# Two window rows mixed in one step, softmax in place, and a plan that counts tiling changes (layer of window attention, linear attention and a recurrent scan)

## The chip, the cores and the metric

The kernel runs on one core of a Trainium2 chip. The core has TensorE (PE in the profile; its weight loads are PEld), VectorE (DVE), ScalarE (ACT), GpSimd (POOL) and SyncE (SP), which here only issues DMAs. SBUF is the on-chip memory; PSUM is the small memory that TensorE writes to. The metric is the device time of one execution in microseconds (us); the time before is the median of three runs.

## What is computed

The input is 16 images of 56 x 56 positions with 128 channels, in fp32. Cut to what matters:

```python
# layer 0: shifted-window attention on the group-normed image
x = x + L0(gn(x))      # roll by -3; qkv; 8 x 8 windows of 7 x 7; 4 heads of 32;
                       # softmax(q k * scale + bias + mask) v; w_out, b_out; roll back
# layer 1, attention part: causal linear attention over the 3136 tokens of an image
q, k = elu(q) + 1, elu(k) + 1
num = einsum(q, cumsum(k v^T));  den = einsum(q, cumsum(k)) + 1e-6
x = x + num / den      # of the layer-normed tokens
# layer 1, ffn part: batch norm over all tokens of (ln(x) @ W.T), then a scan over tokens
y_t = sigmoid(wx_t + y_{t-1} @ V.T)
out = x + y
```

## The kernel before

**Layout.** An image is 3136 tokens. Window attention works on window rows: 7 image rows, 8 windows of 49 positions, all 4 heads; 8 rows an image, 128 in all, in the order 7, 0, 1, ..., 6 (U_ORDER). Linear attention and ffn work on token groups: 6 groups of 512 tokens and one of 64 for each image. The scan at the end runs over all images at once, with 32 segments for each image, and reads what the groups left in DRAM.

**The plan.** Everything before the scan is a list of steps, each with an engine, a cost (busy time, and time until its result may be used), a rank, the steps that it follows, and the buffers that it takes and drops. Plan.run is a list scheduler: each engine takes the ready step of lowest rank whose buffers are free. emit runs it forwards and backwards 200 times with ranks from the run before, keeps the shortest result and writes the instructions out in that order. On the chip each engine follows its own fixed list, with semaphores between engines. The scheduler has one rule on tiled matmuls, which are those that use a part of TensorE's array (scores and mix): while TensorE's last step was a tiled one, another ready tiled step is taken first if its rank lies within NEAR of the lowest ready rank, and entering tiled work from other work adds SWITCH (0.1 us) to a step's cost.

**A window row** (window_row, from L845). ScalarE gathers and normalises the row into x_bufs (L851); TensorE makes q and k (L864) and v (L885), which ScalarE copies out (L869, L878, L897; v has 2 buffers). Scores (L909) are 32 products for each row, of 32 x 49 by 49, each two instructions in fp32, into one of two PSUM pairs (tag "a"). VectorE adds mask and bias into a buffer s (L920, two buffers) and takes maxima (L932), GpSimd subtracts them (L935), ScalarE writes the exponentials to p_bufs (L945, two, chosen by the row's number), VectorE sums (L949, L951), GpSimd scales (L954). TensorE turns the result in eight transposes (L964, step turn), ScalarE copies it to pT (L974, one buffer, 904 elements a partition including gaps). Mix (L983) is 32 products of 49 x 32 by 49, two instructions each. mix_out (L1018) copies the result into oT (one buffer for an image) in four copies, eight where the row wraps around the image's edge. Scores of a row wait for the turn of the row two before.

**A token group** (token_group, from L1210). It needs the window rows that cover its tokens (need, L1576): TensorE projects them (L1234), VectorE adds to the image in xt_bufs (L1243). layer_scale (L1077) normalises tokens. To turn them so that channels lie on partitions, through_dram writes the group to DRAM and reads it back in four pieces in another order (L1058, L1072, SyncE's queue), and VectorE transposes 32 x 32 blocks (L1139); blocks_moved (L1048) says which groups go this way, and the others use TensorE's transposes (L649) and a copy on ScalarE (L1135). There are three such exchanges for a group: the input of the attention ("a"), its keys ("k", L1348 or L1340 and L1344) and the input of the ffn ("f"). Then come features (L1269 to L1292), values (L1317), products (L1372), the running state (L1412, L1424), the attention itself (L1401, L1404), division (L1482) and the update (L1490).

**Start.** Image 0 is turned by TensorE as its groups arrive. Images from 1 on are loaded in another order into the buffer spare (load_turned, load_blocks, L335) in four DMAs; each of them follows the one before it.

Of the kernel before, what the change touches and what calls it, by code (L numbers as in the profile page):

```python
# [15 lines left out]
WS = 7  # L16
# [25 lines left out]
class Step:  # L42


    def __init__(self, engine, cost, rank, emit, after, takes, drops, lag):
        self.engine, self.cost, self.rank, self.emit = engine, cost, rank, emit
        self.takes, self.drops, self.lag = takes, drops, lag
        self.tiles = False
        self.then = []
        self.missing = 0  # L50
        for a in after:
            if a is not None:
                a.then.append(self)
                self.missing += 1


class Plan:
# [11 lines left out]
    SWITCH = 0.1  # L69
    NEAR = 3.0  # L70
# [17 lines left out]
    def run(self, missing, then, rank, gate, begin=None, done=None):  # L88
# [17 lines left out]
        while events:  # L106
# [14 lines left out]
            for e, steps in ready.items():  # L121
                if busy[e]:
                    continue
                held, best = [], None
                if tiles.get(e):
                    near = sorted(r for r in steps if self.steps[r[1]].tiles)
                    for r in near:
                        if r[0] > min(steps)[0] + self.NEAR:
                            break
                        s = self.steps[r[1]]  # L130
                        if begin is None or begin(s):
                            best = s
                            steps.remove(r)
                            heapq.heapify(steps)
                            break
                while steps and best is None:
                    r = heapq.heappop(steps)
                    s = self.steps[r[1]]
                    if begin is None or begin(s):
                        best = s  # L140
                    else:
                        held.append(r)
                for r in held:
                    heapq.heappush(steps, r)
                if best is None:
                    continue
                busy[e] = True
                start[best.n] = t
                more = self.SWITCH if best.tiles and not tiles.get(e) else 0.0
                tiles[e] = best.tiles  # L150
                push(t + more + best.cost, "idle", best)
                push(t + more + best.lag + self.HOP, "done", best)
# [82 lines left out]
def tile_conv_attn_hybrid(  # L235
# [145 lines left out]
    mean_sb = front.tile([P, P], F32, name="mean_sb")  # L381
    nc.gpsimd.memset(mean_sb, 1.0 / C)
    pb_sb = front.tile([P, WT], F32, name="pb_sb")
# [35 lines left out]
    awc_sb = front.tile([P, 3 * P], F32, name="awc_sb")  # L419
# [10 lines left out]
    with ExitStack() as s1:  # L430
# [46 lines left out]
        for i in range(2):  # L477
# [32 lines left out]
        for xt in xt_bufs:  # L510
# [14 lines left out]
                "v": 2,  # L525
                "s": 2,
                "pT": 1,
# [100 lines left out]
        def load_turned(b, rank):  # L628
# [3 lines left out]
            for q in range(4):  # L632
# [6 lines left out]
                        [issued, *parts[-1:]],  # L639
# [193 lines left out]
        last_turn = [None, None]  # L833
# [3 lines left out]
        def window_row(b, u, i, o, t, taken, normed, xw_buf, oT_buf, rank):  # L837
# [4 lines left out]
            kT, v, s, pT = Buf("kT"), Buf("v"), Buf("s"), Buf("pT")  # L842
            asc, apt, apa = Buf("a"), Buf("a"), Buf("a")
            qT = q_bufs[i % 2]
            pr = p_bufs[i % 2]  # L845
# [71 lines left out]
            def masked():  # L917
                d["s"] = own(s, P, 2, NW, WT)
                mask = wmask_sb[:, 1 if u == NU - 1 else 0]
                nc.vector.tensor_tensor(  # L920
                    d["s"].rearrange("p h w k -> p h (w k)"),
                    d["sc"][:, :, 0:UT],
                    mask.rearrange("p w k -> p (w k)")
                    .unsqueeze(1)
                    .to_broadcast([P, 2, UT]),
                    ALU.add,
                )
                d["sf"] = d["s"].rearrange("p h w k -> p (h w) k")

            def maxima():  # L930
                d["mx"] = small.tile([P, nb], F32, tag="mx", name=f"mx_{n}")
                nc.vector.tensor_reduce(d["mx"], d["sf"], AX.X, ALU.max)  # L932

            def minus():
                nc.gpsimd.tensor_tensor(  # L935
                    d["sf"],
                    d["sf"],
# [4 lines left out]
            prf = pr.rearrange("p h w k -> p (h w) k")[:, :, 0:WT]  # L942

            def expo():
                nc.scalar.activation(prf, d["sf"], AF.Exp)  # L945

            def sums():
                d["sm"] = small.tile([P, nb], F32, tag="sm", name=f"sm_{n}")
                nc.vector.tensor_reduce(d["sm"], prf, AX.X, ALU.add)  # L949
# [3 lines left out]
            def scaled():  # L953
                nc.gpsimd.tensor_tensor(  # L954
                    prf, prf, d["rc"].unsqueeze(2).to_broadcast([P, nb, WT]), ALU.mult
# [3 lines left out]
            def turn():  # L959
                pt = pairs[apt.place].rearrange("p h (w q) -> p h w q", w=NW // 2)  # L960
                d["pt"] = pt
                for hp in range(2):
                    for w2 in range(NW // 2):
                        nc.tensor.transpose(  # L964
                            pt[:, hp, w2, 0:NQ2],
                            pr[0:NQ2, hp, 2 * w2 : 2 * w2 + 2, :].rearrange(
# [5 lines left out]
            def turn_out():  # L972
                d["pT"] = own(pT, P, 2, NW // 2, P)
                nc.scalar.copy(d["pT"][..., 0:NQ2], d["pt"][..., 0:NQ2])  # L974

            def mix():
                pa = pairs[apa.place]
                d["pa"] = pa
                for w2 in range(NW // 2):
                    for h in range(HEADS):  # L980
                        for par in range(2):
                            a = 64 * par
                            nc.tensor.matmul(  # L983
                                pa[HD * h : HD * (h + 1), par, w2 * WT : (w2 + 1) * WT],
                                d["v"][a : a + WT, w2, HD * h : HD * (h + 1)],
                                d["pT"][
                                    a : a + WT, h // 2, w2, 64 * (h % 2) : 64 * (h % 2) + WT
                                ],
                                start=True,
                                stop=True,  # L990
                            )

            def mix_out():
# [9 lines left out]
                for par in range(2):  # L1003
                    src = d["pa"][:, par, 0 : UT // 2].rearrange(
                        "p (w i j) -> p w i j", w=NW // 2, i=WS
                    )
                    for i0, y0, m in row_parts(u):
# [13 lines left out]
            xk = st("ACT", (0.48, 0.59), rank, gather_windows, [*taken, *normed, last_value[i % 2]], drops=[xw_buf])  # L1021
# [7 lines left out]
            sc = st("PE", (0.88, 0.95), rank, scores, [q, k, last_turn[i % 2]], takes=[asc], drops=[kT])  # L1029
            last_score[i % 2] = sc  # L1030
            m = st("DVE", (0.88, 0.97), rank, masked, [sc, None if b else made["mask"]], takes=[s], drops=[asc])
            m = st("DVE", (0.87, 0.96), rank, maxima, [m])
            m = st("POOL", (1.47, 1.51), rank, minus, [m])
            e = st("ACT", (0.77, 0.88), rank, expo, [m], drops=[s])
            m = st("DVE", (1.17, 1.26), rank, sums, [e])
            m = st("POOL", (1.48, 1.52), rank, scaled, [m])
            tu = st("PE", (0.77, 0.94), rank, turn, [m], takes=[apt])
            last_turn[i % 2] = tu
            tu = st("ACT", (0.81, 0.92), rank, turn_out, [tu], takes=[pT], drops=[apt])
            mi = st("PE", (0.74, 0.81), rank, mix, [tu, vo], takes=[apa], drops=[pT, v])  # L1040
            sc.tiles = mi.tiles = True
            cost = (0.91, 1.04) if u < NU - 1 else (1.47, 1.65)
# [5 lines left out]
        def blocks_moved(key, b, g):  # L1048

            return key in KEYS and b < B - 1 and g < NG - 1  # L1050
# [26 lines left out]
        def layer_scale(t, g, d, key, rank, after, to, drops=()):  # L1077
# [79 lines left out]
            if blocks:  # L1157
# [3 lines left out]
                    (0.59, 0.68),  # L1161
# [48 lines left out]
        def token_group(b, g, i, t, turned_x, rows_done, oT_buf, xt_buf, rank):  # L1210
# [140 lines left out]
            if blocks_moved("k", b, g):  # L1351
# [4 lines left out]
                    (0.59, 0.68),  # L1356
# [136 lines left out]
            s = st("ACT", part(g, (0.90, 1.00), (0.22, 0.32)), rank, divided, [s], drops=[apn])  # L1493
            up = st("POOL", part(g, (1.02, 1.08), (0.36, 0.42)), rank, update, [s, scaled], drops=[A])
# [65 lines left out]
        for b in range(B):  # L1560
# [7 lines left out]
            for s, u in enumerate(U_ORDER):  # L1568
                rows[u] = window_row(
                    b, u, b * NU + s, o, t, taken, normed, xw_buf, oT_buf, base + SLOT * s  # L1570
                )
            ups, xss, projects = [], [], []
# [417 lines left out]
```

## Time and profile before

| what | us |
|---|---|
| median of 3 runs (lowest, highest) | 1659.29 (1656.67, 1663.87) |
| the profiled execution | 1664.5 |
| its span, first to last instruction | 1661.4 |
| scores, L909: matmul records, mean of one | 8192, 206 ns |
| mix, L983: matmul records, mean of one | 8192, 211 ns |
| turn, L964: records, mean of one | 1024, 261 ns |
| turn_out, L974: copies, mean | 128, 927 ns |
| mix_out, L1018: copies, busy time | 576, 90.9 us |
| mean granted clock of TensorE | 0.994 |

Records of tiled matmuls overlap, so a count times a mean is not the time that a step takes; that is read from the starts of steps in the timeline. The ordinary copies of mix_out are 196 elements (344 ns), 147 (313 ns), 21 (220 ns) and 28 (209 ns) a partition. Busy times of the engines are shares of the whole span; the scan uses TensorE, ScalarE and VectorE in another way than the part before it, so stretches have to be looked at apart.

### The profile page before, as it was taken

The page shows a single profiled execution, that of the slowest core. Times are in us where ns is not written, and L with a number is a line of the kernel's source. Part 1 is how long each engine was busy: PE and PEld are TensorE (multiplying, and loading weights), DVE is VectorE, ACT ScalarE, POOL GpSimd, SP SyncE. Part 2 cuts the span into 40 slices and gives each one's busy share as a digit, 9 for nine tenths or more (in the row PEclk, how much of TensorE's full clock was granted, in tenths as well). Part 3 has the DMA queues.
Part 4 walks back from the last instruction along what each step waited for, and adds up shares of the span by engine and source line. Part 5 has one row for each costly group of instructions (what it writes and reads, how often), then busy time and mean ns, then how long its engine had stood idle before and what let it go on. Part 6 is the DMA issues. An engine that isn't in the chain of part 4 may idle for free.

```text
span 1661.4 us, 63385 instructions
## 1 busy us (share of the span) xinstructions
PE 1615.4 (97%) x25458; PEld 1308.8 (79%) x25459; DVE 1398.1 (84%) x3044; ACT 1183.5 (71%) x3156; POOL 1272.0 (77%) x2154
## 2 busy tenths in 40 slices
PE   7899999999999999999999999999999999999997
PEld 6678787887878887878888778878888887876876
DVE  5779987897989888987979798978898786757997
ACT  5577776777777777777677777767677776766765
POOL 6788978897989898888989889878889786770000
PEclk9999999999999999999999999999999999999999
DMA  5486767677677768586766777776755655558999
GB/s 137 109 186 158 192 151 172 187 167 208 154 204 166 199 153 206 149 208 169 194 165 156 204 168 196 167 191 156 196 148 155 159 160 147 190 183 342 403 419 379
DMA packets 776720, 322.03 MB, mean 194 GB/s; under 512 B 400481, under 2 KB 760161, under 8 KB 774625
## 3 DMA queue, kind: packets, MB, share of 16 engines
q1 hardware_dynamic: 774832, 317.10, 69.9%
q8 instruction: 202, 3.31, 0.9%
q10 hardware_dynamic: 1584, 0.79, 0.2%
q14 instruction: 102, 0.83, 0.2%
HBM read 171.54 MB, written 146.24 MB: 191 GB/s over the span
## 4 chain that ended last, share of the span: by engine, by line
PE 69%; POOL 8%; DVE 7%; SPq 5%; DMA 5%; issue 3%; ACT 2%; DVEq 0%; POOLq 0%; ACTq 0%
PE bank L864 8%; PE bank L1269 8%; PE bank L885 5%; PE pair L909 5%; PE state_bank L1412 4%; PE pair L964 4%; PE pair L1401 4%; PE bank L1317 4%; PE pair L1404 4%; PE bank L1502 4%; PE bank L1372 4%; PE pair L983 4%; SPq L1072 4%; PE bank L1234 4%; PE z_buf L1785 2%
## 5 line engine op out<-in xcount | busy, mean ns | idle before, releaser
L954 POOL TENSOR_TENSOR p_buf<-p_buf,rc 128x784 f32<-128x784 f32 x128 | 194.4, 1519 | 42.7 <-DVE rc L951 14.2
L1269 PE MATMUL bank<-xnT,awc_sb 128*128 128x512 f32 (+1 forms) x448 | 212.9, 557 | 3.3 <-DVE xnT L1139 2.7
L935 POOL TENSOR_TENSOR s<-s,mx 128x784 f32<-128x784 f32 x128 | 192.2, 1502 | 30.8 <-DVE mx L932 28.5
L1279 ACT ACTIVATE r<-bank,bqk_neg 128x512 f32<-128x512 f32 (+1 forms) x224 | 143.4, 640 | 76.9 <-PE bank L1269 67.3
L1412 PEld LDWEIGHTS state_bank<-v_buf,k 128*128 128x128 f32 x768 | 125.4, 191 | 52.1 <-issue 26.7
L1292 DVE SCALAR_TENSOR_TENSOR f<-bank,bqk_one,r 128x512 f32<-128x512 f32 (+1 forms) x224 | 147.5, 658 | 12.6 <-ACT r L1288 12.1
L1412 PE MATMUL state_bank<-v_buf,k 128*128 128x129 f32 x768 | 155.4, 284 | 1.3 <-ACT state L1424 1.1
L974 ACT COPY pT<-pair 128x904 f32<-128x904 f32 x128 | 118.7, 927 | 51.0 <-PE pair L964 41.3
L1401 PE MATMUL pair<-state,f 128*128 128x129 f32 x768 | 153.1, 281 | 0.6 <-issue 0.6
L1424 ACT COPY state<-state_bank 128x129 f32<-128x129 f32 x384 | 107.0, 279 | 65.5 <-PE state_bank L1412 63.9
L1401 PEld LDWEIGHTS pair<-state,f 128*128 128x128 f32 x768 | 123.4, 192 | 37.0 <-issue 21.8
L920 DVE TENSOR_TENSOR s<-pair,wmask_sb 128x784 f32<-128x784 f32 x128 | 122.7, 958 | 34.2 <-PE pair L909 30.0
L909 PEld LDWEIGHTS pair<-kT,q_buf 32*49 32x49 f32 x8192 | 106.4, 121 | 41.9 <-issue 15.7
L949 DVE TENSOR_REDUCE sm<-p_buf 128x16 f32<-128x784 f32 x128 | 121.6, 950 | 18.6 <-ACT p_buf L945 18.3
L1223 POOL TENSOR_TENSOR xt_buf<-xt_buf,bout_sb 128x512 f32<-128x512 f32 (+1 forms) x112 | 129.1, 1158 | 10.7 <-DMA xt_buf<-in_x_dram 10.5
L1788 ACT ACTIVATE y_a<-z_buf,bsh 128x256 f32<-128x256 f32 (+1 forms) x218 | 103.0, 473 | 47.4 <-PE z_buf L1785 43.3
L1288 ACT ACTIVATE r<-r 128x512 f32<-128x512 f32 (+1 forms) x224 | 131.9, 589 | 2.4
L1785 PE MATMUL z_buf<-y_a,fvT_sb 128*128 128x256 f32 (+1 forms) x432 | 131.0, 389 | 0.4 <-ACT y_a L1788 0.4
L909 PE MATMUL pair<-kT,q_buf 32*49 32x49 f32 x8192 | 122.8, 206 | 2.8 <-issue 2.4
L964 PE MATMUL pair<-ident,p_buf 113*128 113x113 f32 x1024 | 120.9, 261 | 3.1 <-POOL p_buf L954 2.8
L964 PEld LDWEIGHTS pair<-ident,p_buf 113*128 113x128 f32 x1024 | 107.5, 142 | 20.5 <-issue 11.2
L932 DVE TENSOR_REDUCE mx<-s 128x16 f32<-128x784 f32 x128 | 121.5, 949 | 0.9
(170 smaller groups left out, 4697.1 us busy)
## 6 DMA issues: line engine op xcount, KB each, us to landing
x_d<-xt_buf SPq DMA_DIRECT2D x96, 256.0 KB, 2.6
xt_buf<-in_x_dram SPq DMA_DIRECT2D x93, 256.0 KB, 3.2
spare<-in_x_dram SPq DMA_DIRECT2D x60, 392.0 KB, 4.5
xs_d<-staged SPq DMA_DIRECT2D x15, 1568.0 KB, 6.9
xna_d<-spare SPq DMA_DIRECT2D x90, 256.0 KB, 2.7
xnk_d<-f SPq DMA_DIRECT2D x90, 256.0 KB, 3.0
xnf_d<-spare SPq DMA_DIRECT2D x90, 256.0 KB, 2.8
spare<-xna_d SPq DMA_DIRECT2D x256, 64.0 KB, 2.1
```

The costliest lines, as they stand in the source:

```text
L864: nc.tensor.matmul(d[key], wqkv_sb[:, j * P : (j + 1) * P], xk, start=True, stop=True)
L909: nc.tensor.matmul(sc[64 * hh : 64 * hh + WT, hp, w * WT : (w + 1) * WT], qT[r : r + HD, w * WT : (w + 1) * WT], d["kT"][r : r + HD, w * W ...
L935: nc.gpsimd.tensor_tensor(d["sf"], d["sf"], d["mx"].unsqueeze(2).to_broadcast([P, nb, WT]), ALU.subtract,)
L954: nc.gpsimd.tensor_tensor(prf, prf, d["rc"].unsqueeze(2).to_broadcast([P, nb, WT]), ALU.mult)
L964: nc.tensor.transpose(pt[:, hp, w2, 0:NQ2], pr[0:NQ2, hp, 2 * w2 : 2 * w2 + 2, :].rearrange("p w k -> p (w k)"), ident[0:NQ2, 0:NQ2],)
L1269: nc.tensor.matmul(d[f"p{j}"], awc_sb[:, j * P : (j + 1) * P], d["xT"][:, :nt], start=True, stop=True,)
L1279: nc.scalar.activation(d[f"r{j}"], d[f"p{j}"], AF.Relu, bias=bqk_neg[:, j : j + 1], scale=-1.0,)
L1288: nc.scalar.activation(d[f"r{j}"], d[f"r{j}"], AF.Exp, scale=-1.0)
L1292: nc.vector.scalar_tensor_tensor(d[key][:, :nt], d[f"p{j}"], bqk_one[:, j : j + 1], d[f"r{j}"], ALU.add, ALU.max,)
L1401: nc.tensor.matmul(to, chunk(d["f0"], cc), t["states"][c], start=True, stop=False)
L1412: nc.tensor.matmul(t["pd"], d["k"][:, cc, :], v1[:, cc, :], start=c == 0, stop=True, skip_group_check=True,)
L1785: nc.tensor.matmul(z, fvT_sb, y_prev, start=False, stop=True, skip_group_check=True)
```

## The change

- **Mix.** Rows are taken in pairs in the order of U_ORDER: (7, 0), (1, 2), (3, 4), (5, 6). The first row of a pair ends with its turn_out; the mix step of the second does both rows, 128 matmul instructions, and writes the two rows' results side by side, so that mix_out copies both at once (pair_parts joins rows that are neighbours in the image). pT gets 2 buffers, v 4. A group that needs the first row of a pair waits for the pair.
- **Softmax in place.** The buffers s are gone. Mask and bias are added into a p buffer; maxima, subtraction, exponential, sums and scaling all work there. There are 3 p buffers, given out by the plan, dropped at the turn. The rule that scores wait for the turn two rows before is gone.
- **turn and turn_out.** The turned pieces are ordered by pair of heads and window pair, and turn_out copies 2 x 49 of each 113 columns, 784 elements a partition. The turn step takes pT.
- **Plan.** tiles becomes 0, 1 (scores) or 2 (mix). ENTER 0.1, LEAVE 0.22 and CHANGE 0.17 replace SWITCH; NEAR goes from 3 to 6, and steps of the same kind come first. Costs of several steps are set anew.
- **Image 0's first two groups** are turned by TensorE for all three keys and not through DRAM.
- **Image 1's four turned loads** no longer follow each other.
- **Room.** mean_sb and pb_sb lie in staged before its first use; awc_sb lies in the unused last 384 columns of xt_bufs[0].

```diff
-    SWITCH = 0.1
-    NEAR = 3.0
+    ENTER, LEAVE, CHANGE = 0.1, 0.22, 0.17
+    NEAR = 6.0
...
-                    near = sorted(r for r in steps if self.steps[r[1]].tiles)
-                    for r in near:
-                        if r[0] > min(steps)[0] + self.NEAR:
-                            break
+                    near = sorted(
+                        (self.steps[r[1]].tiles != tiles[e], r)
+                        for r in steps
+                        if self.steps[r[1]].tiles
+                        and r[0] <= min(steps)[0] + self.NEAR
+                    )
+                    for _, r in near:
...
-                more = self.SWITCH if best.tiles and not tiles.get(e) else 0.0
-                tiles[e] = best.tiles
+                was, tiles[e] = tiles.get(e, 0), best.tiles
+                more = 0.0
+                if was != best.tiles:
+                    more = self.CHANGE if was and best.tiles else self.LEAVE
+                    more = more if was else self.ENTER
...
-        for i in range(2):
+        for i in range(3):
             pb = keep.tile([P, 2, NW, 64], F32, name=f"p_buf{i}")
...
-                "v": 2,
-                "s": 2,
-                "pT": 1,
+                "v": 4,
+                "p": 3,
+                "pT": 2,
...
-                        [issued, *parts[-1:]],
+                        [issued, *(parts[-1:] if b > 1 else [])],
...
+        def pair_parts(u0, u1):
+
+            parts = []
+            for r, u in enumerate((u0, u1)):
+                for i0, y0, m in row_parts(u):
+                    if parts and sum(parts[-1][1:]) == y0:
+                        parts[-1] = (*parts[-1][:2], parts[-1][2] + m)
+                    else:
+                        parts.append((WS * r + i0, y0, m))
+            return parts
...
             def turn_out():
-                d["pT"] = own(pT, P, 2, NW // 2, P)
-                nc.scalar.copy(d["pT"][..., 0:NQ2], d["pt"][..., 0:NQ2])
+                d["pT"] = own(pT, P, NW, 2, WT)
+                nc.scalar.copy(
+                    d["pT"],
+                    d["pt"].rearrange("p n (h q) -> p n h q", h=2)[..., 0:WT],
+                )
...
+                for r, e in enumerate((first_of["d"], d)):
+                    for w2 in range(NW // 2):
+                        for h in range(HEADS):
+                            for par in range(2):
+                                a, c = 64 * par, WT * (2 * w2 + r)
+                                nc.tensor.matmul(
+                                    pa[HD * h : HD * (h + 1), par, c : c + WT],
+                                    e["v"][a : a + WT, w2, HD * h : HD * (h + 1)],
+                                    e["pT"][
+                                        a : a + WT, NW // 2 * (h // 2) + w2, h % 2, :
+                                    ],
+                                    start=True,
+                                    stop=True,
+                                )
...
-            xk = st("ACT", (0.48, 0.59), rank, gather_windows, [*taken, *normed, last_value[i % 2]], drops=[xw_buf])
+            xk = st("ACT", (0.63, 0.73), rank, gather_windows, [*taken, *normed, last_value[i % 2]], drops=[xw_buf])
...
-            sc = st("PE", (0.88, 0.95), rank, scores, [q, k, last_turn[i % 2]], takes=[asc], drops=[kT])
+            sc = st("PE", (0.77, 0.92), rank, scores, [q, k], takes=[asc], drops=[kT])
             last_score[i % 2] = sc
-            m = st("DVE", (0.88, 0.97), rank, masked, [sc, None if b else made["mask"]], takes=[s], drops=[asc])
+            m = st("DVE", (0.88, 0.97), rank, masked, [sc, None if b else made["mask"]], takes=[p], drops=[asc])
...
-            tu = st("PE", (0.77, 0.94), rank, turn, [m], takes=[apt])
-            last_turn[i % 2] = tu
-            tu = st("ACT", (0.81, 0.92), rank, turn_out, [tu], takes=[pT], drops=[apt])
-            mi = st("PE", (0.74, 0.81), rank, mix, [tu, vo], takes=[apa], drops=[pT, v])
-            sc.tiles = mi.tiles = True
-            cost = (0.91, 1.04) if u < NU - 1 else (1.47, 1.65)
+            tu = st("PE", (0.77, 0.94), rank, turn, [m], takes=[apt, pT], drops=[p])
+            tu = st("ACT", (0.72, 0.83), rank, turn_out, [tu], drops=[apt])
+            sc.tiles = 1
+            if i % 2 == 0:
+                first_rows[i] = {"d": d, "u": u, "after": [tu, vo], "drops": [pT, v]}
+                return None
+            first_of = first_rows[i - 1]
+            mi = st(
+                "PE",
+                (1.28, 1.43),
+                rank,
+                mix,
+                [tu, vo, *first_of["after"]],
+                takes=[apa],
+                drops=[pT, v, *first_of["drops"]],
+            )
+            mi.tiles = 2
+            cost = (1.27, 1.42) if first_of["u"] < NU - 1 else (1.90, 2.05)
             return st("ACT", cost, rank, mix_out, [mi], takes=[oT_buf], drops=[apa])
...
-            return key in KEYS and b < B - 1 and g < NG - 1
+            return key in KEYS and b < B - 1 and (b or g >= 2) and g < NG - 1
...
-            up = st("POOL", part(g, (1.02, 1.08), (0.36, 0.42)), rank, update, [s, scaled], drops=[A])
+            up = st("POOL", part(g, (1.22, 1.28), (0.42, 0.48)), rank, update, [s, scaled], drops=[A])
...
+                if s % 2:
+                    rows[U_ORDER[s - 1]] = rows[u]
```

## The prediction

> **What bounds the kernel now.** I read the page's head first, then the busy time by stretches, then TensorE's timeline in the middle of the run, then the chain of waits.
>
> ```profile
> span 1661.4 us, 63385 instructions
> ...
> PE 1615.4 (97%) x25458; PEld 1308.8 (79%) x25459; DVE 1398.1 (84%) x3044; ACT 1183.5 (71%) x3156; POOL 1272.0 (77%) x2154
> ...
> PE   7899999999999999999999999999999999999997
> ```
>
> TensorE has no open time after the second slice. The table of stretches splits the run; the columns are the stretch, its length and the busy time of PE, PEld, DVE, ACT and POOL, with the clock, the DMA share and GB/s last:
>
> ```profile
> 83.00:1411.00 1328.00, 1314.28 (x22314) 1069.01 (x22316) 1141.13 (x2562) 971.88 (x2652) 1141.92 (x1916) 1.00 0.70 175
> 1411.00:1487.00 76.00, 74.94 (x924) 62.64 (x914) 53.23 (x130) 53.03 (x148) 56.51 (x113) 1.00 0.57 192
> 1487.00:1661.00 174.00, 158.63 (x904) 124.11 (x904) 148.67 (x257) 111.90 (x245) 12.96 (x32) 0.97 0.93 374
> ```
>
> For 1328 us TensorE is 99% busy at full clock, VectorE and GpSimd are 86% busy, ScalarE 73%. The last 174 us are the scan, which the change leaves as it is. A busy TensorE can still be a slow one, so I took the time from the start of each of its steps to the start of the next and compared it with the shortest seen for the same step between the same neighbours: from 83 to 1411 us the excess is only 30 us. In the chain of waits from 600 to 700 us nearly every piece is PE. The length of the middle is therefore the sum of TensorE's steps, and an edit counts by what it does to them.
>
> TensorE's timeline shows what a tiled step (scores, L909; mix, L983) costs. Columns: start, time to the end of the last record, engine, line, operation.
>
> ```profile
> 601.78 1.02 PE L1502 MATMUL bank<-xfT,fwTc_sb 128*128 128x512 f32 x2
> 602.73 0.95 PE L909 MATMUL pair<-kT,q_buf 32*49 32x49 f32 x64
> 603.61 0.49 PE L1317 MATMUL bank<-awc_sb,xnT 128*128 128x128 f32 x2
> 603.94 0.39 PE L1412 MATMUL state_bank<-v_buf,k 128*128 128x129 f32 x2
> ...
> 611.12 1.02 PE L1502 MATMUL bank<-xfT,fwTc_sb 128*128 128x512 f32 x2
> 611.98 0.39 PE L1401 MATMUL pair<-state,f 128*128 128x129 f32 x2
> 612.20 0.39 PE L1404 MATMUL pair<-v_buf,A 128*128 128x129 f32 x2
> ...
> 613.09 0.38 PE L1412 MATMUL state_bank<-v_buf,k 128*128 128x129 f32 x2
> 613.40 0.81 PE L983 MATMUL pair<-pT,v 49*32 49x49 f32 x64
> 614.14 1.16 PE L1317 MATMUL bank<-awc_sb,xnT 128*128 128x128 f32 x8
> 615.13 0.82 PE L864 MATMUL bank<-x_buf,wqkv_sb 128*128 128x392 f32 x2
> ...
> 660.73 0.95 PE L909 MATMUL pair<-kT,q_buf 32*49 32x49 f32 x64
> 661.60 0.81 PE L983 MATMUL pair<-pT,v 49*32 49x49 f32 x64
> 662.34 1.12 PE L1269 MATMUL bank<-xnT,awc_sb 128*128 128x512 f32 x2
> ```
>
> Read starts only. L1502 takes 0.86 us ahead of a whole step (611.12 to 611.98) and 0.95 ahead of scores: entering costs 0.09. Scores take 0.88. The step behind, two L1317 matmuls, takes 0.33 where two such matmuls (0.89 for eight) take 0.22: leaving costs 0.10. A mix takes 0.74 between the same edges. Where a mix follows scores at once (661.60), scores keep 0.88 (0.87 here by rounding), the mix 0.74, and one entry and one exit are gone. Over all steps in order, the 256 tiled steps stand in 212 stretches: 28 times a mix follows scores, 16 times scores follow a mix. So a stretch costs 0.196 us over its steps, and 212 of them 42 us.
>
> **The change part by part.**
>
> *Two rows in one mix.* The matmuls stay (64 a row), but 128 steps become 64. Within one mix the records start 6 ns apart for the first 32, then pause, and the last 30 start 8.5 ns apart; 133 ns pass from the last start to the next step. No mix of 128 is in the trace. Low end of the saving: the second row costs a whole 0.74, saving nothing. High end: all of it at 6.3 ns, 0.40 us, saving 64 x 0.34 = 21.6 us. I take the pace of the second half, 64 x 8.5 ns = 0.54, because the first burst looks like a queue that fills once: 64 x 0.20 = **-12.5 us**.
>
> *Fewer stretches.* 192 tiled steps remain. Without any merging there are 192 stretches, saving 20 x 0.196 = 4 us; if every stretch held two steps, 96, saving 23 us. Before, 44 of 256 steps were merged (17%) with a window of 3 us in the plan; it becomes 6 us and the same kind is taken first. I take 52 merges of 192 (27%): 140 stretches, 72 x 0.196 = **-14 us**.
>
> The Trainium skill (TensorEngine Tiling (Array Packing), Key Properties) says that changing the tiling mode drains TensorE, and scores (32 rows by 49 columns) and mix (49 by 32) are different modes, so by this rule putting them side by side would save little. The 28 places where a mix follows scores show no charge beyond the scores' usual 0.88 us; by the rule only the 64 vanished steps would count, 64 x 0.196 = 12.5 us instead of 14, so the sum hardly moves.
>
> *ScalarE.* An ordinary mix_out has copies of 344, 313, 220 and 209 ns, 1.09 us by row; one for two rows, of double width, has about 505 (the 392-wide kT copy is 492), 420, 235 and 230, 1.39: 0.8 us less a pair, 50 us in all. turn_out moves 784 elements, not 904: from 927 ns towards 825 (the slope between 512 elements at 594 and 904 at 927), between 0 and 13 us less. I count **nothing**: ScalarE is 73% busy and TensorE's steps cover it. If that cover were gone, up to 60 us would come off ScalarE's own 972.
>
> *Softmax in place, buffers.* Reading the strided p_buf costs VectorE no more (sums 950 ns against maxima 949) and GpSimd 17 ns (1519 against 1502), 2 us over 128 rows. The strided write by the mask's sum is not in the trace; between nothing and, by that GpSimd pair, 1%, 1.2 us. Both are under TensorE's cover. The rule that scores of row i wait for the turn of row i-2 goes; masked waits for the turn of row i-3, and behind it on VectorE stand the other groups' steps. Turn now needs a free pT on TensorE itself, but what frees it is an earlier mix on the same engine, so no foreign wait is added there. **0**, within the stalls below.
>
> *Start.* Six exchanges through DRAM vanish (two groups, three keys): 30 DMA issues from SyncE's queue, 6 x (0.4 + 2.0) = 14 us of it, and in their place 24 transposes and 6 copies: 24 x 0.11 = 2.7 us of TensorE, 3.6 of ScalarE. The four loads of the turned image 1 no longer wait for each other:
>
> ```profile
> 18.80 3.17 SPq L335 DMA_DIRECT2D spare<-in_x_dram  x1
> 48.11 0.39 SPq L1058 DMA_DIRECT2D xna_d<-spare  x1
> 50.52 2.02 SPq L1072 DMA_DIRECT2D spare<-xna_d  x4
> 52.58 0.43 SPq L335 DMA_DIRECT2D spare<-in_x_dram  x1
> ```
>
> One of them stands at 18.80, the next shown at 52.58, and image 1's first transposes (L683) come at 68. TensorE is open for 15.5 of the first 83 us; 7 of its excess lie there, the rest before any row exists. Bounds: +3 (transposes on a full engine) to -7. I take **-3**.
>
> *Plan costs and stalls.* The new costs are nearer to the records (update 1.22 against 1.16 measured where it had 1.02; gather 0.63 against 0.75, had 0.48), which could take some of the 30 us of stalls: low end -10. Against it, VectorE keeps its work while the middle shrinks by 25: its idle time falls from 187 to 162 us, 13%, and by the same share the stalls grow by **+4**. High end +20.
>
> Sum: -12.5 - 14 - 3 + 4 = -25.5, so 1661.4 becomes 1636 in the profiled span. That execution took 1664.5 in all and the median of the runs is 1659.29; I take the difference off the median: **1634**. The terms' own ends, not all at once, give 1623 to 1643.
>
> **Rivals.**
>
> *The output buffer waits for the pair (slower).* There is one oT buffer; its first copy for an image comes 0.3 to 6.4 us after the last projection of the one before in images 4 to 15 (743.5 to 750.0 for image 8). With pairs the first copy needs the image's second row too, and that row's turn came 10, 9 and 7 us after the release in images 7 to 9. If TensorE ran out of other work for 3 us at each of 15 boundaries, 45 us would be lost: 1634 + 45 = 1679. It decides from 25.5 / 15 = 1.7 us a boundary. Against it: the first projection of an image needs the second row before as well, and it started 16 to 22 us after the release; v goes from 2 to 4 buffers and p to 3, so rows can run ahead. 12%.
>
> *Hidden behind VectorE and GpSimd.* Both reach 88% of a shorter middle, in order; new stalls eat all but a few us: 1656, within 0.5%. For it: seven pieces of 1.5 us of GpSimd's p_buf (L954) are among the longest pieces of the chain. Against: nearly all of the chain in the middle is TensorE. 6%.
>
> *Half.* The double mix keeps its burst-and-pause twice (saving near 0) and merges stay at 17% (159 stretches, 10.4 us): -10.4 - 3 + 4, 1649. 15%.
>
> *More.* As forecast, and the truer costs halve the 30 us of stalls: -25.5 - 4 - 15, 1615. This also covers better merging. 12%.
>
> **How the numbers follow.** The forecast has 55%. Faster by over 0.5% (8.3 us, about what a measurement of this kernel tells from no change): 55 + 15 + 12 = 82%; within: 6%; slower: 12%. From 1616 to 1654 lie the forecast, the half case and part of the other two.
>
> **What would show it.** Mix in 64 steps of 128 at 1.28 us from start to start; about 140 stretches of tiled steps; ScalarE's mix copies 320 instead of 576 and its busy time near 1125; the middle 22 to 25 us shorter with TensorE still at 99%; image 1's first transposes before 60 us. A mix at 1.45, stretches over 170, or TensorE's stalls over 50 us would make it wrong, and gaps of more than 2 us at each image's boundary would show the first rival.

## The result, and the profile after

The changed kernel takes 1667.52 us (median of 14 runs) where the kernel before takes 1662.76 us (14 runs beside it): a ratio of 1.0032, with a 95% interval of 1.0017 to 1.0047. The change makes the kernel a little slower, by about 5 us. The forecast was 1634 us, 25 us faster.

The head of the profile page after looks as the one before did: span, busy time by engine, TensorE's slices.

```profile
span 1664.3 us, 63157 instructions
...
PE 1602.6 (96%) x25483; PEld 1309.3 (79%) x25483; DVE 1393.3 (84%) x3038; ACT 1161.8 (70%) x2906; POOL 1273.8 (77%) x2155
...
PE   8999899999999999999999999999999999999997
```

TensorE is busy for 13 us less, and the span is 3 us longer. The table of stretches says where the open time is (columns as in the prediction):

```profile
83.00:1411.00 1328.00, 1296.05 (x22059) 1060.72 (x22058) 1134.07 (x2541) 942.81 (x2395) 1139.31 (x1908) 0.99 0.69 172
1411.00:1487.00 76.00, 75.29 (x1067) 63.94 (x1066) 53.33 (x129) 54.48 (x150) 56.78 (x113) 1.00 0.58 194
1487.00:1661.00 174.00, 159.53 (x923) 124.98 (x921) 149.97 (x263) 113.31 (x251) 15.03 (x38) 0.98 0.94 376
```

In the middle TensorE stood open for 13.7 us before and 32.0 now, and its clock is 0.99 where it was 1.00. No other engine took over: VectorE and GpSimd are less busy too. The list of TensorE's waits after (engine, line, what was waited for, total us, times, longest) names the new open time:

```profile
PE pair L925 <- issue: 16.0, 8, 5.2
PE pair L1002 <- issue: 8.8, 7, 2.8
PE bank L655 <- DMA xt_buf<-in_x_dram: 4.4, 1, 4.4
PE pc L1938 <- DVE seam_count L1934: 3.5, 1, 3.5
```

L925 is scores and L1002 the mix. Before, the mix had no "issue" in this list, and scores (L909) had 2.4 us:

```profile
PE pair L909 <- issue: 2.4, 3, 1.0
```

The third and fourth line were there before (4.5 and 3.5 us). "Issue" is time for which no semaphore and no other engine answers. TensorE's timeline shows where it falls, inside a step:

```profile
186.82 1.02 PE L1300 MATMUL bank<-xnT,xt_buf 128*128 128x512 f32 x2
187.68 1.05 PE L1403 MATMUL bank<-f,f 128*128 128x128 f32 x8
188.57 0.39 PE L1265 MATMUL bank<-wout_sb,oT_buf 128*128 128x128 f32 x2
188.89 1.38 PE L1002 MATMUL pair<-pT,v 49*32 49x49 f32 x128
190.20 0.57 PE L925 MATMUL pair<-kT,q_buf 32*49 32x49 f32 x31
195.99 0.98 PE L925 MATMUL pair<-kT,q_buf 32*49 32x49 f32 x33 [5.22 <-issue]
196.90 2.08 PE L1300 MATMUL bank<-xnT,xt_buf 128*128 128x512 f32 x2
198.77 1.75 PE L901 MATMUL bank<-wqkv_sb,x_buf 128*128 128x128 f32 x8
```

A scores step stops after 31 of its 64 matmuls, all of whose operands are there, for 5.2 us. It follows a mix of 128. And the steps behind it go at half speed: L1300 takes 1.87 us from start to start where it took 0.86 ahead of the gap (186.82 to 187.68), L901 1.58 instead of 0.89. The trace has the granted clock (the share of full speed at which TensorE is let run) at one half for 6.8 us from 193.4 on; in this row, third number from the end, the first 0.4 us are still at full speed:

```profile
193.00:197.00 4.00, 1.01 (x34) 0.92 (x34) 0.00 (x0) 0.00 (x0) 1.74 (x3) 0.55 0.75 217
```

A lack of instructions would stop an engine without a semaphore, and the profile has a queue for these (packets, MB, share of 16 engines' time; the line reads the same before and after):

```profile
q8 instruction: 202, 3.31, 0.9%
```

202 packets of 3.31 MB are 16 KB each. TensorE's records of all kinds (matmuls, weight loads, semaphores) number 51,215, which makes 254 a packet. I take a packet for a page of 256 instructions, and the next count bears that out. Counting the records in order, all 15 gaps over 0.35 us inside tiled steps come at the same place, number 193 modulo 256, and so do the 3 of before. This place is called the border of a page here. At this one place the gaps (over 0.25 us, ahead of the scan) sum to 33.0 us after and 7.3 before; at all other places of a tiled step there is next to nothing.

That gives the theory which the experiments test. *TensorE's instructions come in pages of 256, and only one page ahead.* In the trace a fetch starts a median of 0.9 us after a border is crossed (in a quarter of the cases before it, by up to 2.7 us), takes 1.05 (0.88 to 1.6), and TensorE can cross the next border 1.23 to 1.40 us after the fetch has landed. That floor holds throughout: in the traces of the two kernels and of all runs below, some 200 borders in each, no border was crossed sooner than 1.19 us after that landing. It makes a median of some 3.4 us (5 to 95%: 0.9 to 5.4) from one border to the earliest crossing of the next. Most pages last longer than that: 173 of 199 in this trace took over 3.5 us, and 4 of these had a gap over 0.3 us behind them; of the 26 faster ones 16 had. A pair's mix is 256 instructions (128 matmuls and as many weight loads) in 1.31 us, a page by itself, and scores behind it make 384 in 2.2 us. Sixteen pages of after hold mix and scores alone and last under 1.7 us; 23.7 us of gaps stand behind them. Before had two such pages, and 0.1 us. Taking each gap as "landing of the fetch plus 1.3 us, less the time at which the page before is used up" gives 30.6 us for after where 31.3 are measured in the 17 gaps above 0.3 us, and 5.4 for before where 5.7 are; it is this measure of the gaps that is given for every run below.

The Trainium skill (Runtime: NRT & Kernel Launch, Instruction fetch mechanics) also has refills of 256 instructions, and calls crossing a border "mostly hidden". The size agrees with the 202 packets of 16 KB; "hidden" held for before (5.7 us) and does not hold here (31.3).

### The profile page after: what moved, and what is told of

The parts are those of the page before. It is cut to its first block, busy times and chain, and to the rows that moved or that the text cites. A ratio compares the mean times of both kernels' runs of the same rounds, so it can differ in the third digit from the quotient of the medians.

```text
span 1664.3 us, 63157 instructions
## 1 busy us (share of the span) xinstructions
PE 1602.6 (96%) x25483; PEld 1309.3 (79%) x25483; DVE 1393.3 (84%) x3038; ACT 1161.8 (70%) x2906; POOL 1273.8 (77%) x2155
## 3 DMA queue, kind: packets, MB, share of 16 engines
q8 instruction: 202, 3.31, 0.9%
## 4 chain that ended last, share of the span: by engine, by line
PE 77%; DVE 6%; POOL 6%; DMA 4%; issue 4%; SPq 2%; ACT 0%; DVEq 0%; POOLq 0%; ACTq 0%
PE bank L880 9%; PE bank L1300 9%; PE bank L901 6%; PE pair L925 6%; PE pair L979 5%; PE state_bank L1443 5%; PE bank L1265 5%; PE pair L1432 5%; PE bank L1403 5%; PE bank L1348 5%; PE pair L1435 5%; PE pair L1002 5%; PE bank L1533 4%; PE z_buf L1818 2%; DVE z_buf L1806 2%
## 5 line engine op out<-in xcount | busy, mean ns | idle before, releaser
L949 POOL TENSOR_TENSOR p_buf<-p_buf,mx 128x784 f32<-128x784 f32 x128 | 194.5, 1520 | 42.6 <-DVE mx L946 30.1
L1300 PE MATMUL bank<-xnT,xt_buf 128*128 128x512 f32 (+1 forms) x448 | 212.5, 557 | 2.3 <-DVE xnT L1170 0.8
L937 DVE TENSOR_TENSOR p_buf<-pair,wmask_sb 128x784 f32<-128x784 f32 x128 | 122.9, 960 | 36.4 <-PE pair L925 32.2
L925 PEld LDWEIGHTS pair<-kT,q_buf 32*49 32x49 f32 x8192 | 106.7, 120 | 47.0 <-issue 32.2
L925 PE MATMUL pair<-kT,q_buf 32*49 32x49 f32 x8192 | 123.8, 206 | 16.0 <-issue 16.0
L989 ACT COPY pT<-pair 128x784 f32<-128x784 f32 x128 | 104.8, 818 | 32.1 <-PE pair L979 31.2
L957 ACT ACTIVATE p_buf<-p_buf 128x784 f32<-128x784 f32 x128 | 113.2, 884 | 14.0 <-POOL p_buf L949 13.4
```

The costliest lines, as they stand in the source:

```text
L925: nc.tensor.matmul(sc[64 * hh : 64 * hh + WT, hp, w * WT : (w + 1) * WT], qT[r : r + HD, w * WT : (w + 1) * WT], d["kT"][r : r + HD, w * W ...
L949: nc.gpsimd.tensor_tensor(d["prf"], d["prf"], d["mx"].unsqueeze(2).to_broadcast([P, nb, WT]), ALU.subtract,)
L1300: nc.tensor.matmul(d[f"p{j}"], awc_sb[:, j * P : (j + 1) * P], d["xT"][:, :nt], start=True, stop=True,)
```

## The experiments

Rivals of this theory: the stall belongs to the mix and scores themselves (operands, ports, the change of tiling), or the new order of steps is worse for some other reason. What tells them apart is moving the borders while the order stays, and the order while the steps stay. Ratios are to the kernel before, measured beside each run.

**The same order, borders moved by 64 instructions.** 32 small matmuls are put ahead of the plan.

```diff
+        for _ in range(32):
+            nc.tensor.matmul(state_bank, ident16[:, 0:P], ident16[:, 0 : C + 1], start=True, stop=True)
```

> Edit: 32 matmuls in bf16 ahead of the first load's arrival, 64 instructions of TensorE more, in time that it idles; the plan and the order of all else are those of the changed kernel. Theory F: the borders of 256 instructions fall 64 instructions earlier in the program, so other steps stall; every gap over 0.35 us inside a tiled step is again at one and the same position modulo 256, and the sum of the border gaps is anywhere between 15 and 45 us: 1650 to 1680. Rival P: the same steps stall as in the changed kernel, and the time is 1667 within 3 us.

1659.56 us, ratio 0.9982 (0.9959 to 1.0004). The gaps moved to other steps, and all 17 inside tiled steps are at number 193 again. Their sum stays, 31.0 us. The time at half clock ahead of the scan fell from 27.3 to 20.5 us, which makes at most 3.4 us; the rest of the difference to after is not explained.

**Borders moved by 200.**

```diff
+        for _ in range(100):
+            nc.tensor.matmul(state_bank[:, 0:2], ident16[:, 0:P], ident16[:, 0:2], start=True, stop=True)
```

> Edit: the changed kernel's order, with 100 two-column bf16 matmuls at the start, borders 200 instructions earlier; the first transposes may start 1 to 3 us late. Theory F: the replay over the changed kernel's starts gives 45 to 63 us of gaps, the worst position, against 28 to 38 unmoved: 1667.5 + 20 + 2 = about 1690, ratio 1.017. Rival P: 1667 to 1671, ratio 1.004.

1710.29 us, ratio 1.0254 (1.0212 to 1.0296). Nothing differs but 100 matmuls of two columns, and the kernel is 43 us slower than after. Its waits of TensorE:

```profile
PE pair L931 <- issue: 27.9, 11, 4.9
PE pair L1008 <- issue: 18.6, 14, 2.5
```

Gaps sum to 59.8 us, as expected, and some 68 us ahead of the scan run at half clock; the time is 20 us above the 1690 expected, which had put too little on the clock. Where a border lies in a step decides, so the steps' operands don't.

**Scores and mixes kept apart.** A step that is not tiled is taken after a tiled one.

```diff
-                        (self.steps[r[1]].tiles != tiles[e], r)
+                        (0, r)
                         for r in steps
-                        if self.steps[r[1]].tiles
+                        if not self.steps[r[1]].tiles
```

> Edit: after a tiled step the plan looks for a step that is not tiled, where the changed kernel looks for another tiled one. Tiled steps then stand in 191 stretches instead of 167: 24 x 0.196 = +4.7 us of TensorE work. Theory F (instruction supply: TensorE loses time where its instruction stream crosses a border of 256 instructions, because pages of nothing but tiled matmuls are used up in about 1.4 us, faster than the next page comes): the gaps at those borders fall from 33 us to under 10, and the time at half clock that follows long gaps from 27 us to about 10, so 1667.5 + 4.7 - 23 - 6 = about 1643, ratio 0.988 to the kernel before. Rival P (the loss is in the new order: waits on VectorE, GpSimd or the oT buffer): nothing falls, 1667.5 + 4.7 = 1672, ratio 1.006.

1654.02 us, ratio 0.9950 (0.9927 to 0.9972). With 191 stretches of tiled steps in place of 167 the kernel is faster than before, if by half a percent. That merging, meant to save, costs isn't shown by it alone: the same order with the borders elsewhere gains nothing (below). And gaps of 21.3 us are left, more than was expected, with one merge left of 25: a pair's mix has as many instructions as a page without any merge.

**The same edit in the kernel before.** There `near` is `sorted(r for r in steps if not self.steps[r[1]].tiles)`.

> Edit: the kernel before with the same rule as in apart (after a tiled step one that is not tiled). Stretches go from 212 to 252: 40 x 0.196 = +7.8 us. Theory F: border gaps, 7.3 us before, fall below 4, half clock a little less: 1662.8 + 7.8 - 4 - 2 = about 1665, ratio 1.001. Rival P: 1662.8 + 7.8 = 1671, ratio 1.005.

1677.56 us, ratio 1.0101 (1.0069 to 1.0132): a miss, slower than either. Its gaps are 9.8 us, more than the 5.7 of before and not less, and its 252 stretches cost by count 40 x 0.196 = 8 us more than 212. That makes some 12 of the 16 us. The theory had the direction of the gaps wrong here, at a size of 4 us.

**The start as before.** Image 0's first groups go through DRAM again and image 1's loads follow each other, the rest as after.

```diff
-                        [issued, *(parts[-1:] if b > 1 else [])],
+                        [issued, *parts[-1:]],
...
-            return key in KEYS and b < B - 1 and (b or g >= 2) and g < NG - 1
+            return key in KEYS and b < B - 1 and g < NG - 1
```

> Edit: of the changed kernel, image 0's first two groups go through DRAM again and image 1's four loads follow each other again; the rest stays (the plan comes out in another order, with 160 stretches). Theory F: with 32 adjacent tiled steps instead of 25 the border gaps are 33 x 32/25 = about 42 us, less 7 x 0.196 = 1.4 us of work; the first 83 us hold 4 us less TensorE work, as before the change: 1667.5 + 9 - 1 + 4 = about 1679, ratio 1.010. Rival P: the start alone counts, 1667.5 + 4 - 1 = 1670.

1694.91 us, ratio 1.0215 (1.0162 to 1.0268). That is beyond both expectations. The planner found another order, 13 us longer by its own reckoning (1467 us against 1454), with 49.7 us of gaps and 44 us at half clock. It says nothing on the start alone, and shows how much a new order can move the gaps.

**One mix a row, the rest of the change kept.**

```diff
-                for r, e in enumerate((first_of["d"], d)):
+                for r, e in ((0, d),):
...
-            mi = st("PE", (1.28, 1.43), rank, mix, [tu, vo, *first_of["after"]], takes=[apa], drops=[pT, v, *first_of["drops"]])
+            mi = st("PE", (0.63, 0.78), rank, mix, [tu, vo], takes=[apa], drops=[pT, v])
```

> Edit: the changed kernel with the pairing alone undone, a mix and a mix_out for each row as before; softmax in place, buffers, plan rules, start and costs stay. 214 stretches instead of 167 (+9 us) and the second row's full price (64 x 0.16 = +10 us): 20 us more work. Theory F: no step fills a page alone; border gaps fall from 32 to about 10 us and half clock by 10 us (-5): 1667.5 + 20 - 22 - 5 = about 1660, ratio 0.999. Rival P: 1667.5 + 20 = 1687, ratio 1.015.

1660.16 us, ratio 0.9977 (0.9960 to 0.9993), as theory F had it. A mix of 64 is half a page. Gaps are 5.7 us, as before the change, and the middle is busy again:

```profile
83.00:1411.00 1328.00, 1313.91 (x22390) 1067.82 (x22390) 1140.68 (x2551) 959.20 (x2636) 1144.72 (x1910) 1.00 0.69 172
```

So the pair's mix brings the gaps, not the new buffers, the softmax in place or the start; nor is it the merging alone, as 42 of 256 tiled steps are merged here and 25 of 192 in after. This run also has another order and other borders, so luck with these is a rival. A replay of the recorded starts speaks against it: take the gaps out, put the borders at each of 64 places, and let a page be usable 3.0 us after the border before it. It gives 2 to 10 us of gaps for this order and 19 to 45 for that of after (an estimate; with 3.4 us 5 to 16 and 27 to 62). Less their gaps, singles would take 1660.2 - 5.7 = 1654.5 and after 1667.5 - 31.3 = 1636.2: by this estimate, which leaves the clock aside, the pairing without gaps is worth about 18 us.

**A plan that counts instructions.** Each TensorE step carries its count (scores 128, mix 256, an ordinary step 4 to 16); a border comes every 256, and can be crossed 3.6 us after the last. A step that would be held 0.1 us or more gives way to one that would not. The plan also gets a wider window (NEAR 12), other look-ahead times (AHEAD) and 300 passes.

```diff
+        def held_up(s, t):
+
+            count = s.count * (1 + self.EXTRA)
+            left, free, late = self.PAGE - page[0] % self.PAGE, page[1], 0.0
+            while left <= count:
+                at = t + late + s.cost * left / count
+                late += max(0.0, free - at)
+                free = max(at, free) + self.READY
+                left += self.PAGE
+            return late, free
...
+                        if begin is not None and self.paging and held_up(s, t)[0] >= 0.1:
+                            continue
```

> Edit: the plan counts TensorE's instructions and models their supply: the border of each 256 can be crossed 3.6 us after the one before at the earliest; a step that would be held up there by 0.1 us or more gives way to the next in rank that isn't. NEAR 12, the look-ahead times 40, 25, 15, 8. Theory F (supply of instructions at borders of 256): the plan has 173 stretches, +6 x 0.196 = 1.2 us of work, and counts on 3 us of hold-ups; border gaps fall from about 32 us to under 12, the time at half clock before the scan from 27 us to under 14 (-6): 1667.5 + 1 - 20 - 6 = about 1643, ratio 0.988 to the kernel before. Rival P (the loss is in the order and in waits on other engines): no gain, 1667 or more, ratio 1.003.

1646.77 us, ratio 0.9887 (0.9864 to 0.9911), with 16.6 us of gaps where under 12 were expected.

**The same order, borders 128 instructions earlier.** 64 two-column matmuls ahead of that plan, which doesn't know of them.

> Edit: paged's order to the last step, with 64 two-column bf16 matmuls at the start, so that every border of 256 falls 128 instructions earlier than the plan reckoned with. Theory F: the replay of moved borders over paged's recorded starts gives 42 to 56 us of gaps against 6 to 10 unmoved (16.6 measured); with the half clock that follows, 1647 + 35 = about 1682, ratio 1.011. Rival P (paged is faster because its order happens to be a better one): the order is the same, 1647 to 1651, ratio 0.989 to 0.991.

1688.41 us, ratio 1.0155 (1.0126 to 1.0184), with 49.5 us of gaps. This is the clearest of the runs: one order of steps, the same matmuls behind 64 tiny ones, and 42 us between them by where the page borders fall (33 us of gaps and, with some 55 us at half clock in place of 10, up to 22 us of slower work). The gain of the counting plan therefore hangs on where the borders lie: with them elsewhere its order, wider window and all, is slower than the kernel before.

**The kernel with scores and mixes apart, borders moved** by 56 two-column matmuls, to where a replay of its order with a fixed time per page had fewest gaps.

> Edit: apart's order, with 56 two-column bf16 matmuls ahead of the first load's arrival, so that all borders of 256 fall 112 instructions earlier in the program. Theory F: moving the borders over apart's recorded starts, with the next page usable 3.0 to 3.4 us after a border, gives 9 to 17 us of gaps where the same replay gives 20 to 31 unmoved: 1654 - 12 = about 1642, ratio 0.988. Rival P: the order is the same, 1654 within 4 us, ratio 0.995.

1663.25 us, ratio 0.9990 (0.9977 to 1.0003), gaps 26.5 us: a miss. One time for all fetches doesn't forecast such a sum to 10 us. Nor did the time stay, as the rival had it: in the same order it rose by some 7 us (by ratio, 0.9950 to 0.9990).

**The counting plan tuned.** Borders put 16 instructions later, 4.2 us from border to border, NEAR 9, AHEAD 50, 35, 20, 12.

> Edit: paged with the borders put 16 instructions later, where paged's own trace has them (the replay puts its 16.6 us of gaps down to that offset), 4.2 us for a page instead of 3.6, NEAR 9, look-ahead times 50, 35, 20, 12. Theory F: 176 stretches, 3 more than paged (+0.6 us); gaps from 16.6 to under 7 us: 1647 - 9 = about 1638, ratio 0.984. Rival P: no systematic change, 1647 within 6 us, ratio 0.989.

1640.84 us, ratio 0.9873 (0.9851 to 0.9896). The same kernel once more, and beside it one with 3.6 us and AHEAD 30, 20, 10, 5:

> The same kernel as paged_fit, for a profile, since the one taken there was of a disturbed execution. Theory F: border gaps under 7 us, half clock ahead of the scan under 10 us, time 1641 within 3, ratio 0.987. Rival P: gaps as in paged, about 17 us, and the time explained by something else.

> Edit: as paged_fit with 3.6 us for a page and the look-ahead times of the changed kernel; 172 stretches (-0.8 us). Theory F: with less reserve for a page (in the traces a page can be entered 3.4 us after the one before at the median, over 3.9 in a quarter of the cases) the gaps are 6 to 15 us, so 1641 + 5 = about 1646, ratio 0.990. Rival P: 1641 within 6 us in either direction.

1641.09 us, ratio 0.9870 (0.9846 to 0.9893), and 1644.94 us, ratio 0.9909 (0.9881 to 0.9937). Gaps are 7.5 and 13.0 us. The first misses its expectation a little, in gaps (under 7) and in half clock (13.6 us, under 10). Its list of TensorE's waits, with mix L1060 and scores L983, answers to the one of after:

```profile
PE bank L713 <- DMA xt_buf<-in_x_dram: 4.5, 1, 4.5
PE pair L1060 <- issue: 3.9, 4, 1.4
PE pc L1996 <- DVE seam_count L1992: 3.5, 1, 3.5
PE pair L983 <- issue: 2.3, 3, 1.6
```

24.8 us of "issue" in scores and mix have become 6.2. The stretches show that more of the work is done by 1411 us: 22,594 matmuls in place of 22,059, so that 590 are left for the second stretch in place of 1067.

```profile
83.00:1411.00 1328.00, 1315.17 (x22594) 1077.14 (x22593) 1150.42 (x2589) 961.15 (x2444) 1159.08 (x1946) 1.00 0.70 174
1411.00:1487.00 76.00, 71.34 (x590) 56.30 (x590) 50.56 (x130) 51.05 (x142) 46.08 (x101) 1.00 0.71 255
```

This is the fastest version: 19 us under the kernel before measured beside it, and further under the changed one. On the scale of the runs first shown it makes 0.987 x 1659.29 = 1638 us, close to the 1634 that was forecast with instructions taken as free. As another plan made it, that closeness isn't evidence for the forecast's terms.

## Why the prediction was wrong

**What bounds the kernel.** Rightly read as TensorE's steps, and still so. But the sentence "the length of the middle is therefore the sum of TensorE's steps" took the rate of instructions for free, and that is the step that failed: no term of the sum asks how fast the instructions themselves can come. The trace had the answer in it: three gaps inside scores steps at one place modulo 256, and 202 packets of 16 KB on a queue of their own. With the gaps between steps they cost 5.7 us. Those between steps were counted among the "30 us of stalls"; the three inside steps, some 3 us, weren't counted at all, as the measure takes a step that is cut in two for two steps. In the sum the step that failed stands as the term of stalls: +4 forecast, +25.6 measured in gaps and up to 8.5 in clock.

**Two rows in one mix: -12.5 forecast, -10.4 measured.** Away from a gap the step takes 1.31 us from start to start (1.28 forecast):

```profile
601.89 1.38 PE L1002 MATMUL pair<-pT,v 49*32 49x49 f32 x128
603.20 0.49 PE L1432 MATMUL pair<-state,f 128*128 128x129 f32 x2
```

Two single ones take 1.476, so it saves 64 x 0.162 us. The mechanism was right; what was not seen is that the same step, at 195 instructions a microsecond, outruns its supply.

**Fewer stretches: -14 forecast, -8.8 by count.** There are 167, not 140: of 192 steps 25 are merged, 12 mixes after scores and 13 scores after mixes; 45 x 0.196 = 8.8 us. The wider window merged a smaller share than the old one (13% against 17%). And it is where a mix and scores stand side by side that the 16 pages of nothing else arise.

**Stalls: +4 forecast, +25.6 measured in gaps at the borders**, and 17 us more at half clock (27.3 against 10.2 ahead of the scan), which costs up to half of that, 8.5. The forecast sought stalls among VectorE, GpSimd and buffers; no such wait grew to a size that counts in the list of TensorE's waits.

**Start: -3.** Image 1's first transposes (L689) come at 36.9 us, before the 60 asked for, and the loads no longer follow each other. TensorE is busy for 71.7 us of the first 83 where it was for 67.5. Of these 4.2 us 2.7 are new work, so 1.5 are left as a gain, and part of them may be slower work, at half clock. What the start is worth in the whole was not isolated.

**ScalarE, softmax in place: 0, as forecast.** Mix copies are 320, turn_out 818 ns (825 forecast, 927 before); ScalarE's 1161.8 us are above the 1125 named, as mix copies went from 90.9 us of busy time to 69.8, by 21 and not by 50: copies of one row overlap (four take 0.72 us in the timeline before), and the forecast had added their means. TensorE's cover hid it. The mask's sum, now a strided write, takes 960 ns against 958.

The account of the span: -10.4 - 8.8, some -1.5 from the start, +25.6 and 0 to +8.5 make +5 to +13; measured +2.9. The 2 to 10 us between are not explained.

**The rivals.** The oT buffer does wait for the pair: in front of image 7 its first copy comes 22.9 us after the last projection. But TensorE had other work, as the stretch between them shows:

```profile
643.40:666.30 22.90, 21.28 (x316) 16.71 (x315) 16.43 (x38) 16.32 (x44) 20.26 (x37) 1.00 0.84 221
```

So that rival named a place at which nothing much is lost, and the slower outcome came by another. VectorE and GpSimd did not become the bound either. "Half" had the merges nearly right (159 stretches; 167 came) and the mix wrong. Of the signs listed as showing the forecast wrong, one came. The mix is not at 1.45 and the stretches are not over 170, but TensorE's stalls are over 50 us: the time over the shortest of the same step between the same neighbours is 34 us, and the 28 us of gaps inside steps, which that measure leaves out as they cut a step in two, make it 62 (31 and 3, so 34, before). The gaps stand at page borders and not at the images' boundaries.

## What to carry to other kernels

Where steps of very short matmuls are joined or put side by side, count instructions as well as time: 256 instructions in under 1.5 us mostly had a gap behind them here (13 pages of 16), and the time saved in the array was given back in waiting for pages. A gap inside a step, with no semaphore behind it, is worth placing by its number in the engine's own sequence before it is put down to operands. A planner that orders steps can put slow steps between the dense ones once it counts, and here it got back some 25 us of the changed kernel's time.

## What the runs showed of the hardware

- **Pages.** Gaps of TensorE lie at one place modulo 256 instructions in the runs, wherever the steps were moved (25 of 25 inside tiled steps with borders moved by 200, 28 of 28 by 128, 19 of 21 with the old start). Each border waits for the landing of one fetch, which starts within a few us of the border before (median 0.9 us after it), and never came sooner than 1.19 us behind that landing; this fits one page fetched ahead.
- **How long a page takes varies**, from 0.9 to 5.4 us from a border to the earliest crossing of the next (5 to 95%). A fetch starts later in the busier microseconds of the DMA queues (0.2 us after the border with queues under 30% busy, 1.5 us with full ones). That is a correlation of 0.42 and was not tested.
- **Half clock after short gaps.** Over all traces 41 of 72 gaps of 1.7 to 3 us had 3.4 or 6.8 us at half clock begin in them or within 3.4 us behind them, as at 50.0 us in after with a gap of 2.8; of 95 gaps of 1.0 to 1.7 us three had. The Trainium skill (TensorE: Matmul & The Clock Gate, What's actually happening) has a window of about 3.4 us, after which an idle engine's clock is halved; the lengths of 3.4 and 6.8 us agree with such a window, but here gaps well short of one were enough.
- **Luck in a schedule.** Two kernels that differ by 100 two-column matmuls ahead of the plan are 43 us apart. A difference of 1% between two orders of a kernel this dense may say nothing of the change that made them.
